# Two more places in the queue of small steps between a block's tokens and the turn of its normalised tokens

## The chip, the cores and the metric

The kernel runs on one core of one Trainium2 chip. The metric is the device time of one execution in microseconds (us), where lower is better. Each kernel is run several times; the time before is the median of three runs. One further execution was recorded by the hardware profiler, and everything said here of engines, waits and orders comes from that record.

The engines are named as the profile names them: PE (TensorE, the matrix unit), PEld (its weight loads), DVE (VectorE), ACT (ScalarE), POOL (GpSimd) and SP (SyncE, which here only issues transfers). [...]

## The reference

The input is four images of 128 channels by 4096 positions, in float32. Layer 0 group-normalises an image, makes queries and keys of 64 channels, values and a gate, attends over all positions, gates, projects and adds the input:

```python
vg = sigmoid(conv_bn(x, Wvg, svg, bvg)); v, gate = split(vg)
attn = softmax(einsum('bdn,bdm->bnm', q, k))
out = einsum('bcm,bnm->bcn', v, attn) * gate
x = x + conv_bn(out, Wp, sp, bp)
```

Layer 1 works on tokens (position by channel). It attends with queries that are their own keys, adds, normalises each token, and feeds the normalised tokens into a recurrence that runs over the positions:

```python
q = ln(t) @ W;  t = t + softmax(q @ q.T) @ ln(t)
Wx = batch_norm(ln(t) @ W_f.T)
y[n] = sigmoid(Wx[n] + y[n-1] @ V.T);  t = t + y
```

The queries of layer 1 are their own keys, so the score matrix is symmetric, and the kernel computes only half of its blocks.

## The kernel before, in words

All that counts here is in the function `fast`. For each of the four images it runs `layer0` and then `layer1`; after the last image comes the recurrence, as a scan over short pieces.

`layer0` goes over 8 blocks of 512 queries, each with 16 pairs of key tiles. A pair is two score matmuls (line 200), one exponential (ACT, line 202), a running sum (DVE, line 209) and four weighing matmuls (line 383).

`layer1` goes over the same 8 blocks in the order 6, 7, 5, 4, 3, 2, 1, 0, and in block n over the key blocks n, n-1, ..., 0. Each key block is two half steps. A half step is two score matmuls (line 573), two exponentials (ACT, line 579), two 32x32 block turns on DVE (line 584), and the two direct products of two half steps earlier (line 463). After a key block other than n itself, SP issues sixteen transfers that complete the turn of the scores (line 605). Some half steps later `reversed_products` uses the turned scores (four matmuls, line 476, a sum on DVE, line 481) for the mirrored block. So a query block is complete when its own products and all mirrored ones have arrived; then `finish(n)` runs.

Beside this main stream there are small steps, held in two queues. `pending` holds the steps that finish a block. `ahead` holds the 38 steps that prepare the next image for layer 0: four `stats`, `mean`, `variance`, and then per chunk of 512 positions `normalise`, `queries_keys`, `values` and `gate`. A half step of layer 1 takes one small step: the first of `pending`, or, if that is empty, the first of `ahead` (lines 598 to 601). Layer 0 takes from `ahead` first, then from `pending`, there in every second pair only, or in each pair while more than six are waiting (lines 215 to 218). The prepared image's queue is filled before its predecessor's layer 1 begins, and is empty in the last image.

`finish(n)` in layer 1 puts four steps into `pending`:

- `tokens`: the softmax sum's reciprocal, four PE transposes of the block into the tile `mt` (line 519), four DVE instructions that scale and add the old tokens into `t1b` (line 521), and a layer norm: statistics on DVE (lines 256, 257), the reciprocal root on POOL (lines 116, 117), and four DVE instructions that write the normalised tokens `h2` (line 260; the profile names this tile `h` or by its buffer).
- `result`: four PE transposes of `t1b` into `mr` (line 531), an ACT copy (line 533), a transfer to DRAM (line 534).
- `turn`: four PE transposes of the normalised tokens into `mh` (line 539), an ACT copy into `th` (line 540).
- `inputs`: one matmul of `th` into `mw` (line 544), statistics and a copy on DVE (lines 545, 551), a transfer to DRAM (line 552).

All small steps that need PSUM share one bank, the pool `ps_m`, which has one buffer under the one tag `m`: `mt`, `mr`, `mh`, `mw`, and `mp` of the steps for the next image (`queries_keys` at line 315, read by DVE 319, ACT 323 and DVE 327; `values` at 335, read by DVE 340; `gate` at 350, read by ACT 351).

The source order is not the final one. A scheduler reorders instructions on each engine when the program is built, following the dependencies, the buffers and its own idea of durations. So an edit of the source can move instructions that it doesn't mention.

The function `nothing` is a place holder. Layer 0 already uses it twice in its own list of finishing steps (line 430), where it does nothing and costs a place.

## Time and profile before

| | |
|---|---|
| median of three runs | 3160.87 us (3160.32 to 3160.97) |
| profiled execution: span | 3157.6 us |
| PE busy | 3071.5 us, 97% |
| DVE busy | 1792.3 us, 57% |
| ACT busy | 1128.2 us, 36% |
| POOL busy | 141.4 us, 4% |

The span is counted from the first to the last instruction. A matmul of 512 float32 columns appears as two records. The records overlap, [...] so the distance from one start to the next tells more than the length of a record. A line of the profile gives a source line, an engine, the tiles written and read, a count, the busy time with the mean of one, and after the bar the time that the engine was idle before these instructions and what ended that time.

### The profile page before, as it was taken

How to read it: one execution, taken by the hardware profiler on the slowest of the kernel's cores; microseconds unless marked ns; L12 is line 12 of the kernel's file. 1: busy time of each engine (PE TensorE's matmuls, PEld its weight loads, DVE VectorE, ACT ScalarE, POOL GpSimd, SP SyncE). 2: the span in 40 equal slices, each digit the busy share in tenths (PEclk: the TensorE clock that was granted, in tenths of full speed). 3: DMA queues.
4: the chain of work that ended last, by engine and by line, in shares of the span. 5: the costliest groups of instructions: out<-in, count | busy, mean ns of one | idle time of the engine just before them, and what ended most of it. 6: DMA issues, size and time to landing. Idle time of an engine off the chain costs nothing.

```text
span 3157.6 us, 32263 instructions
## 1 busy us (share of the span) xinstructions
PE 3071.5 (97%) x10770; PEld 1374.8 (44%) x10770; DVE 1792.3 (57%) x2964; ACT 1128.2 (36%) x1986; POOL 141.4 (4%) x183
## 2 busy tenths in 40 slices
PE   7999999999999999999999999999999999999976
PEld 3444444444444444444444444444444444444433
DVE  6555556555555555655555555555555655454546
ACT  3433333333333333333333333333333333223324
POOL 0000000000000000000000000000000000000000
PEclk9999999999999999999999999999999999999988
DMA  1111133333111123334211113333321112443324
GB/s 50 37 44 54 54 100 93 92 90 92 48 50 51 54 70 91 96 87 98 70 54 51 54 45 98 93 93 93 88 53 54 54 48 72 136 105 89 98 87 169
DMA packets 233167, 241.14 MB, mean 76 GB/s; under 512 B 88480, under 2 KB 144288, under 8 KB 231968
## 3 DMA queue, kind: packets, MB, share of 16 engines
q1 hardware_dynamic: 231984, 238.18, 27.2%
q8 instruction: 89, 1.46, 0.2%
q10 hardware_dynamic: 1008, 0.79, 0.1%
q14 instruction: 86, 0.70, 0.1%
HBM read 65.80 MB, written 56.62 MB: 39 GB/s over the span
## 4 chain that ended last, share of the span: by engine, by line
PE 91%; DVE 4%; POOL 1%; DMA 1%; SPq 1%; issue 1%; ACT 1%; ACTq 0%; DVEq 0%; POOLq 0%
PE o L383 28%; PE ps L200 15%; PE o L463 14%; PE ps L573 13%; PE ot L476 12%; PE mt L409 1%; PE mq L424 1%; PE mw L544 1%; PE md L227 1%; PE mp L315 1%; PE ps_r L719 1%; PE mh L539 1%; POOL rstd L117 1%; DVE t1b L521 1%; PE mp L350 1%
## 5 line engine op out<-in xcount | busy, mean ns | idle before, releaser
L383 PE MATMUL o<-e,nxt 64*128 64x512 f32 x4096 | 963.8, 589 | 0.0
L202 ACT ACTIVATE e<-ps 128x1024 f32<-128x1024 f32 x512 | 521.2, 1024 | 742.7 <-PE ps L200 738.1
L209 DVE TENSOR_TENSOR acc<-acc,e 128x1024 f32<-128x1024 f32 x448 | 546.4, 1220 | 387.9 <-ACT e L202 376.6
L579 ACT ACTIVATE e<-ps,shift 128x512 f32<-128x512 f32 x580 | 394.0, 684 | 776.4 <-PE ps L573 486.2
L383 PEld LDWEIGHTS o<-e,nxt 64*128 64x128 f32 x4096 | 398.9, 187 | 482.4 <-issue 474.6
L573 PE MATMUL ps<-qt 128*128 128x512 f32 x1160 | 550.4, 595 | 3.0 <-ACT e L579 3.0
L200 PE MATMUL ps<-nxt 64*128 64x512 f32 x2048 | 540.9, 602 | 1.2 <-DVE nxt L327 0.9
L463 PE MATMUL o<-e,h 128*128 128x512 f32 x1160 | 537.0, 592 | 0.0
L476 PE MATMUL ot<-tt,h 128*128 128x512 f32 x888 | 401.5, 595 | 5.3 <-DMA tt<-dd 5.3
L584 DVE STREAM_TRANSPOSE dd<-e 128x512 f32<-128x512 f32 x444 | 286.1, 685 | 110.8 <-ACT e L579 57.3
L463 PEld LDWEIGHTS o<-e,h 128*128 128x128 f32 x1160 | 218.4, 190 | 262.1 <-issue 261.2
L573 PEld LDWEIGHTS ps<-qt 128*128 128x128 f32 x1160 | 213.2, 191 | 244.4 <-issue 224.2
L200 PEld LDWEIGHTS ps<-nxt 64*128 64x128 f32 x2048 | 189.5, 186 | 248.0 <-issue 162.7
L476 PEld LDWEIGHTS ot<-tt,h 128*128 128x128 f32 x888 | 168.3, 191 | 217.1 <-issue 212.4
L481 DVE TENSOR_REDUCE slots<-tt 128x4 f32<-128x2048 f32 x111 | 250.6, 2258 | 11.3 <-DMA tt<-dd 11.2
L490 DVE TENSOR_TENSOR oacc<-oacc,ot 128x512 f32<-128x512 f32 x87 | 59.3, 682 | 209.5 <-PE ot L476 209.5
L116 POOL TENSOR_SCALAR rstd<-mv 128x4 f32<-128x4 f32 x64 | 14.6, 228 | 2519.5 <-DVE mv L257 2519.5
L579 ACT ACTIVATION_READ_ACCUMULATOR e<-ps,shift 128x1 f32 x580 | 113.9, 196 | 0.0
L401 POOL TENSOR_SCALAR xb<-xb,bpc 128x512 f32<-128x512 f32 x32 | 54.3, 1698 | 318.0 <-DMA xb<-in_x_dram 285.2
L117 POOL TENSOR_TENSOR rstd<-rstd,mhalf 128x4 f32<-128x4 f32 x64 | 66.4, 1038 | 5.3
L719 PE MATMUL ps_r<-y,w 128*128 128x256 f32 x168 | 54.4, 443 | 9.8 <-ACT y L716 7.8
L260 DVE TENSOR_SCALAR h<-t,mv,rstd 128x128 f32<-128x128 f32 x128 | 35.7, 343 | 45.3 <-POOL rstd L117 45.3
(124 smaller groups left out, 1411.8 us busy)
## 6 DMA issues: line engine op xcount, KB each, us to landing
tt<-dd SPq DMA_DIRECT2D x1776, 64.0 KB, 2.0
turn_d<-d SPq DMA_DIRECT2D x96, 256.0 KB, 2.0
t_d<-t SPq DMA_DIRECT2D x64, 256.0 KB, 2.0
nxt<-in_x_dram SPq DMA_DIRECT2D x16, 512.0 KB, 5.8
xb<-in_x_dram SPq DMA_DIRECT2D x32, 256.0 KB, 2.9
t<-turn_d SPq DMA_DIRECT2D x128, 64.0 KB, 2.0
yt<-turn_d SPq DMA_DIRECT2D x128, 64.0 KB, 1.9
ht<-turn_d SPq DMA_DIRECT2D x128, 64.0 KB, 2.0
```

Of the source, the lines that this page charges most:

```text
L117: nc.gpsimd.tensor_tensor(dst, dst, mhalf[:, :n], ALU.pow)
L200: nc.tensor.matmul(ps[:, h, :], lhsT=lhsT, rhs=rhs, start=True, stop=True)
L202: nc.scalar.activation(e, ps, AF.Exp, scale=scale)
L209: nc.vector.tensor_tensor(acc, acc, e, ALU.add)
L383: nc.tensor.matmul(o[r], lhsT=v[rs, p + h * PAIRS, :], rhs=e[rs, h, :], start=(p == 0 and h == 0), stop=(p == PAIRS - 1 and h == 1),)
L463: nc.tensor.matmul(o, lhsT=h[:, NQ * a + 2 * i + half, :], rhs=e[:, half, :], start=(a == order(n)[0] and i == 0 and half == 0), stop=(a = ...
L476: nc.tensor.matmul(ot, lhsT=h[:, NQ * n + j, :], rhs=t[:, :, j, :, :].rearrange("q p k j -> q k p j"), start=(j == 0), stop=(j == NQ - 1),)
L481: nc.vector.tensor_reduce(slots[:, bass.ts(n, NQ), a], t.rearrange("q p b k j -> q b p (k j)"), AX.XY, ALU.add,)
L573: nc.tensor.matmul(ps[:, half, :], lhsT=qt[:, bass.ts(at, P)], rhs=qt[:, bass.ts(n, QB)], start=True, stop=True,)
L579: nc.scalar.activation(e[:, half, :], ps[:, half, :], AF.Exp, bias=shift, accum_out=slots[:, at, n : n + 1],)
L584: nc.vector.transpose(d.rearrange("q f b k j -> q k b f j")[:, 2 * i + half], e[:, half, :].rearrange("q (b f j) -> q b f j", b=NQ, f=NQ),)
L719: nc.tensor.matmul(bank(k, s), lhsT=wt["vt"], rhs=before, start=False, stop=True, skip_group_check=True,)
```

## The change

Two edits. The place holder `nothing` now runs the first step of `ahead`, if there is one. And `finish` of layer 1 puts two such place holders between `result` and `turn`; in the last image only for the blocks 4 to 7.

```diff
         def nothing():
-            pass
+            if ahead:
+                ahead.popleft()()
...
                 if b == B - 1 and n == 0:
                     pending.extend([tokens, turn, inputs, result])
+                elif b == B - 1 and n < 4:
+                    pending.extend([tokens, result, turn, inputs])
                 else:
-                    pending.extend([tokens, result, turn, inputs])
+                    pending.extend([tokens, result, nothing, nothing, turn, inputs])
```

No instruction is added or removed on any engine; all that changes is their order. The place holders in layer 0's own list change too: where they come up in layer 1, at the start of an image's second layer, they also run a step of `ahead`.

## The prediction

> **What bounds the kernel now.** I read the page first, then who waits for whom on PE, then the timeline of PE around single turns.

> ```profile
> span 3157.6 us, 32263 instructions
> ...
> PE 3071.5 (97%) x10770; PEld 1374.8 (44%) x10770; DVE 1792.3 (57%) x2964; ACT 1128.2 (36%) x1986; POOL 141.4 (4%) x183
> ...
> PE 91%; DVE 4%; POOL 1%; DMA 1%; SPq 1%; issue 1%; ACT 1%; ACTq 0%; DVEq 0%; POOLq 0%
> ```

> The chain that ends last (third line) runs on PE for 91% of the span. No PE instruction is removed, so only PE's pauses can be won, and PE is idle for 86.1 us (3157.6 - 3071.5) in all, start and end included. The list of PE's waits says where:

> ```profile
> PE mh L539 <- DVE h L260: 15.7, 21, 4.4
> PE gm L292 <- DVE gmv L290: 14.2, 1, 14.2
> ...
> PE ot L476 <- DMA tt<-dd: 5.3, 3, 3.0
> PE ps L573 <- ACT e L579: 3.0, 6, 0.8
> PE mh L539 <- ACT e L579: 2.8, 3, 1.0
> ```

> The turn's transposes (line 539) waiting for the layer norm's last DVE step (line 260) are the largest entry. The second is one wait at the program's start. The timeline of image 0's block 7 shows one turn:

> ```profile
> 597.63 0.60 PE L531 MATMUL mr<-ident,t1b 128*128 128x128 f32 x4
> ...
> 598.07 1.88 PE L463 MATMUL o<-e,h 128*128 128x512 f32 x4
> ...
> 599.03 1.04 POOL L117 TENSOR_TENSOR rstd<-rstd,mhalf 128x4 f32<-128x4 f32 x1
> ...
> 600.10 1.11 DVE L260 TENSOR_SCALAR h<-t1b,mv,rstd 128x128 f32<-128x128 f32 x4 [1.48 <-POOL rstd L117]
> ...
> 600.60 0.49 PE L539 MATMUL mh<-ident,h 128*128 128x128 f32 x2 [0.65 <-DVE h L260]
> ```

> PE has four matmul records (1.72 us at 0.43 from start to start) for the time in which POOL takes the root and DVE writes the first normalised quarter. They end at 599.79 and the turn starts at 600.60: 0.81 us lost. From `result`'s first transpose to the turn's first is 2.97 us here and 2.1 to 3.3 us in image 0's other stalled turns; that is the distance needed.

> [...] records of 592 ns start 429 ns apart, so I count from start to start. [...] so one waiting transpose holds the main stream behind it, as at 600.60. [...] one queries/keys result is read by DVE (0.80 us), ACT (0.77) and DVE (0.82), one after the other. [...]

> **The change part by part.** Nothing is removed or added on any engine; the built program holds the same instructions in another order, and layer 0 of image 0 is untouched.

> *Moved later: `turn` and `inputs`.* Four transposes (0.11 us apart, 0.44), an ACT copy (0.59), a matmul of two passes (0.86), DVE statistics and copy (0.69 each), one transfer. None costs more at its new place, except that one group per image more falls between layer 0's matmuls, where a change of shape costs about 0.09 us on each side (520 against 429 ns): 0.2 us an image, 0.6 in all. On SP the transfer of line 552 stands 32 instead of 16 score transfers behind that of line 534. [...] PE waited for scores 3 times only (5.3 us), all in image 3 before its first `finish`, where this transfer doesn't exist. I take nothing.

> *The gain.* In the built order of PE I count the matmuls between `result` and `turn` at 0.43 us a pass. Image 0, in order of blocks 6, 7, 5, 4, 3, 2: before 1.9, 1.9, 1.9, 1.9, 1.1, 1.9 us; after 9.7, 5.4, 10.5, 6.2, 7.9, 9.7. All exceed the 3.3 us needed. Start to start, those six turns lost, with the gaps between their transposes, 0.85, 0.8, 0.95, 0.85, 0.8 and 1.1: 5.35 us. Blocks 1 and 0 lose nothing before (5.4 us of work). Block 7 keeps about 0.5 (next part). So 4.8 us an image, 14.4 for three. In image 3 the built order separates block 6 (8.8 us) and block 7 (4.5) but leaves 1.9 us in blocks 5 and 4, although their places were moved: 0.85 + 0.75 won, 1.6. Sum 16.0 us.

> *Moved earlier: the next image's steps.* They now use the bank between `result` and `turn`. The bank is free about 1.1 us after `mr`'s end, and about 1.0 after a gate's. In two turns an image the step follows with 0.86 us of work, 0.2 us each; the old order had two such gate pairs as well, so I put 0.2 more. In block 7's turn `queries_keys` comes in, and its reads stand behind the layer norm on DVE: first read at about 3.6 us after `mr`'s start (600.10 + 1.11 - 597.63), the three reads done at 6.0, where PE comes to `turn` at 5.6 to 5.9: the 0.5 kept above covers these. ACT's read waits as well, with exponentials behind it for about 2.9 us; PE has two score buffers and some 3.4 us of work, so I add nothing.

> *The cluster of the first chunks.* With the queue two or more places further on, its order changes about 40 us into layer 1. Before, PE lost time there so:

> ```profile
> 476.81 1.12 PE L573 MATMUL ps<-qt 128*128 128x512 f32 x2 [0.76 <-ACT e L579]
> ...
> 484.23 2.84 PE L573 MATMUL ps<-qt 128*128 128x512 f32 x6 [0.25 <-ACT e L579]
> ...
> 487.37 1.16 PE L335 MATMUL mp<-w,nxt 128*128 128x128 f32 x8 [0.29 <-DVE nxt L340]
> ```

> Start to start these are 0.92, 0.42 and 0.46: 1.8 us, 1.9 with small gaps. In the new order a `values` group stands directly behind a `queries_keys` matmul, with no PE work between. These lines price it:

> ```profile
> 477.77 1.02 PE L315 MATMUL mp<-nxt,w 128*128 128x512 f32 x2
> ...
> 478.83 0.80 DVE L319 TENSOR_SCALAR nxt<-mp,par 64x512 f32<-64x512 f32 x1 [2.03 <-PE mp L315]
> ...
> 479.67 0.77 ACT L323 ACTIVATE nxt<-mp,par 64x512 f32<-64x512 f32 x1 [2.91 <-DVE nxt L319]
> ...
> 480.48 0.82 DVE L327 TENSOR_SCALAR nxt<-mp,par 64x512 f32<-64x512 f32 x1 [0.84 <-ACT nxt L323]
> ```

> From the second pass's end (478.63) to the third read's end (481.30) are 2.7 us, in which PE now stands. With 0.3 for exponentials in a queue, the cluster costs 3.0 us: 1.1 more an image, 3.3 for three. Bounds: below, the DVE queue may run ahead and the whole cluster cost no more than before (0); above, the two score waits come on top (1.3 more an image).

> *Layer 0's edge.* Image b+1's first block now ends while a transpose of image b's last block still holds the buffer of `og`, so line 392 starts about 0.6 us later. In the trace the block's two sums are freed 2.1 us after the last weighing matmul; with 0.6 added this meets PE's need for a third buffer at about 2.9. Zero taken, at most 0.7 an image.

> *The steps that fall into layer 0's old place holders* (two `stats`) stand at the same place on DVE as before, the scheduler having drawn them ahead already. The mean and variance chain moves before a score turn on DVE (line 584), which may start about 3 us later; DVE was idle 8.9 us just before it. Zero.

> Sum: 16.0 - 0.6 - 0.6 (the 0.2 for gates, three images) - 3.3 = 11.5 us, so the profiled span would be 3146. The three runs lie about 3.3 us above the span; the difference is set off against their median: 3160.9 - 11.5 = 3149.4, rounded 3149.

> **The rivals.**
> - *Whole gain.* The cluster costs what it did, and block 7's turn waits for nothing: 16.0 + 1.5 - 0.6 = 17, so 3144. For it: DVE is busy 57% only. Against: the serial three reads are in the trace.
> - *The wait moves to the bank.* The new users of the one bank take back most of it: the cluster at its upper bound (4.0 more in three images), layer 0's edge at its bound (2.1), 0.5 more for blocked exponentials in each of three turns (1.5): 11.5 - 7.6 = 4, so 3157. For it: ACT's order puts exponentials behind a read that waits for DVE.
> - *Slower, by starved scores.* If an exponential queued behind a small step's read holds up the score matmuls for 1.5 us in each of the six turns of three images (18 turns, 27 us), the sum is 15 us slower, 3176. It decides from 0.64 us a turn (11.5 / 18). For it: PE waited for exponentials for up to 0.8 us in the old cluster. Against: in the turns ACT is 36% busy and there are matmuls of 3 us and more between.
> - *The change does nothing where meant.* The built order leaves blocks 5 and 4 of image 3 as they were; for images 0 to 2 it does separate them, so only that remainder (1.7 us) stays.

> **How the numbers follow.** Chances: forecast (3146 to 3153) 0.55, whole gain (3141 to 3146) 0.17, moved wait (3153 to 3161) 0.20, slower 0.08. About 0.2%, 6.3 us, is what a measurement of this kernel can tell from no change. Faster than 3154.5 takes the first two and a fifth of the third: 0.76. The rest of the third is same, 0.16; slower 0.08. The range leaves out half of the whole gain's case at its far end, a little of the moved wait's, and the slower case: 3142 to 3160. The forecast's own range is 3146 to 3153.

> **What would show it.** Right: line 539's idle time falls from 18.5 us to about 7 (the last block's 4.4 us, block 5 and 4 of image 3 and a little of block 7), PE's busy time is unchanged, and a wait of lines 335 or 315 for DVE line 327 appears, 2 to 3 us in each of three images. Wrong: the idle time of line 539 stays; or scores (line 573) wait for ACT for more than 6 us in all; or `ot` waits for transfers in images 0 to 2.

## The result, and the profile after

The changed kernel takes 3147.1 us (median of four runs, 3144.93 to 3148.81) against 3160.85 (3160.32 to 3160.97): 13.75 us less, a ratio of 0.9956 with an interval of 0.9939 to 0.9974. The profiled execution spans 3144.8 us, 12.8 less than that of before. Lines after line 170 of the source stand 3 further down now, those after the second edit 5: the turn's transposes are line 542, the layer norm's last step 263, the bank's third read 330, `values` 338, the scores 578.

The page of the kernel after: span, busy time, and the chain that ends last.

```profile
span 3144.8 us, 32242 instructions
...
PE 3064.3 (97%) x10770; PEld 1379.2 (44%) x10770; DVE 1798.6 (57%) x2964; ACT 1125.5 (36%) x1986; POOL 142.0 (5%) x183
...
PE 94%; DVE 3%; SPq 1%; DMA 1%; POOL 0%; ACT 0%; issue 0%; ACTq 0%; DVEq 0%; POOLq 0%
```

The same 10770 matmuls run, and PE's share of the chain rises from 91% to 94%: what went away is standing time. PE's busy time fell by 7.2 us, where the prediction had it unchanged. The record of a pass is longer than the distance to the next start (592 against 429 ns), so up to 0.16 us of each pause counts as busy; of the 12.8 us only 5.6 show as idle time (80.5 us, before 86.1). Who waits for whom on PE (total us, times, longest):

```profile
PE mp L338 <- DVE nxt L330: 7.7, 3, 2.6
PE mh L542 <- DVE h L263: 6.5, 4, 4.4
...
PE ot L479 <- DMA tt<-dd: 4.7, 3, 3.0
```

The turn's wait (18.5 us with the part that was put down to ACT) is down to 6.5, of which 4.4 are the last block of all. The waits of scores for ACT (3.0 us in six places) are off the list of the costliest. A new entry stands above the turn's: `values` waits for the third read of the small bank, once in each of the first three images. The timeline of PE around block 7's turn in image 0:

```profile
596.04 0.60 PE L534 MATMUL mr<-ident,t1b 128*128 128x128 f32 x4
596.47 1.02 PE L466 MATMUL o<-e,h 128*128 128x512 f32 x2
597.35 1.12 PE L318 MATMUL mp<-nxt,w 128*128 128x512 f32 x2
598.32 1.88 PE L578 MATMUL ps<-qt 128*128 128x512 f32 x4
600.03 1.88 PE L466 MATMUL o<-e,h 128*128 128x512 f32 x4
602.05 0.66 PE L542 MATMUL mh<-ident,h 128*128 128x128 f32 x4
```

Twelve passes stand between `mr` and `mh` where there were four, the bank's new user (line 318) among them, and the distance is 6.0 us. The last product before the turn needs 1.72 us from start to start, and the turn starts 2.02 us after it (602.05 - 600.03), so 0.3 us are still lost: the bank holds the turn up, whose first weight load waits 0.97 us for the third read (line 330). The place of the new wait, in image 0, all engines but PEld:

```profile
489.12 1.07 PE L318 MATMUL mp<-nxt,w 128*128 128x512 f32 x2
490.23 0.80 DVE L322 TENSOR_SCALAR nxt<-mp,par 64x512 f32<-64x512 f32 x1 [1.22 <-PE mp L318]
491.07 0.77 ACT L326 ACTIVATE nxt<-mp,par 64x512 f32<-64x512 f32 x1 [2.91 <-DVE nxt L322]
491.88 0.82 DVE L330 TENSOR_SCALAR nxt<-mp,par 64x512 f32<-64x512 f32 x1 [0.84 <-ACT nxt L326]
...
492.75 1.16 PE L338 MATMUL mp<-w,nxt 128*128 128x128 f32 x8 [2.56 <-DVE nxt L330]
```

Three reads, one after the other, and nothing for PE to do: this is the sequence that the prediction priced at 2.7 us. It is 2.56 us of idle time; counted from start to start 2.72 are lost. The third read takes the other 64 partitions than the second and still waits for ACT (0.84 us in the trace); what asks for that isn't shown.

In image 1 the same pause has a sequel. The timeline of PE there:

```profile
1238.06 1.07 PE L318 MATMUL mp<-nxt,w 128*128 128x512 f32 x2
1241.68 1.32 PE L338 MATMUL mp<-w,nxt 128*128 128x128 f32 x8 [2.56 <-DVE nxt L330]
1242.80 5.17 PE L479 MATMUL ot<-tt,h 128*128 128x512 f32 x8
```

Eight records of `ot` take 5.17 us; eight such records take 3.60 elsewhere. The table of stretches of 3.41 us around the pause names the cause: the first two are of image 0, the next two of image 1, the last two of image 2 (after the times: length, busy time of PE, PEld, DVE, ACT and POOL with counts, TensorE's granted clock with 1.00 for the full one, DMA share, GB/s).

```profile
488.19:491.60 3.41, 2.00 (x5) 0.49 (x3) 1.62 (x2) 0.53 (x1) 0.00 (x0) 1.00 0.45 109
491.60:495.01 3.41, 2.26 (x11) 1.57 (x12) 1.88 (x3) 0.58 (x2) 0.00 (x0) 1.00 0.24 58
1239.13:1242.54 3.41, 0.86 (x7) 0.86 (x8) 1.62 (x2) 0.77 (x1) 0.00 (x0) 1.00 0.41 100
1242.54:1245.95 3.41, 3.41 (x7) 1.61 (x6) 2.90 (x3) 0.63 (x1) 0.00 (x0) 0.50 0.02 5
1990.06:1993.47 3.41, 1.17 (x9) 1.17 (x10) 1.34 (x2) 0.77 (x1) 0.00 (x0) 1.00 0.39 96
1993.47:1996.88 3.41, 3.41 (x5) 1.38 (x5) 3.38 (x3) 0.63 (x1) 0.00 (x0) 0.50 0.02 5
```

In images 1 and 2 the granted clock falls to half for 3.4 us, beginning about 1 us after the pause's end. In image 0 the pause is as long, and the clock stays. The last section returns to these lines.

The cleanest measure of what each kernel wins is the time from the first score of one image's layer 1 to that of the next image's, called an image's time from here on. Before it is 754.2 us in each of three images; now it is 748.9 us in image 0 and 750.6 in images 1 and 2, where the half clock costs 1.7.

### The profile page after: what moved, and what is told of

Its sections match the earlier page's. It is cut to its first block, busy times and chain, and to the rows that moved or that the text cites. A ratio compares the mean times of both kernels' runs of the same rounds, so it can differ in the third digit from the quotient of the medians.

```text
span 3144.8 us, 32242 instructions
## 1 busy us (share of the span) xinstructions
PE 3064.3 (97%) x10770; PEld 1379.2 (44%) x10770; DVE 1798.6 (57%) x2964; ACT 1125.5 (36%) x1986; POOL 142.0 (5%) x183
## 4 chain that ended last, share of the span: by engine, by line
PE 94%; DVE 3%; SPq 1%; DMA 1%; POOL 0%; ACT 0%; issue 0%; ACTq 0%; DVEq 0%; POOLq 0%
PE o L386 28%; PE ps L578 15%; PE o L466 15%; PE ps L203 15%; PE ot L479 12%; PE mq L427 1%; PE mt L412 1%; PE md L230 1%; PE mw L547 1%; SPq L610 1%; PE ps_r L724 1%; PE mp L318 1%; PE mp L338 1%; PE mp L353 1%; PE mh L542 1%; DVE ps_r L711 1%
## 5 line engine op out<-in xcount | busy, mean ns | idle before, releaser
L484 DVE TENSOR_REDUCE slots<-tt 128x4 f32<-128x2048 f32 x111 | 250.7, 2258 | 11.7 <-DMA tt<-dd 11.6
L116 POOL TENSOR_SCALAR rstd<-mv 128x4 f32<-128x4 f32 x64 | 14.4, 225 | 2525.0 <-DVE mv L260 2525.0
L117 POOL TENSOR_TENSOR rstd<-rstd,mhalf 128x4 f32<-128x4 f32 x64 | 66.4, 1037 | 5.3
```

Of the source, the lines that this page charges most:

```text
L117: nc.gpsimd.tensor_tensor(dst, dst, mhalf[:, :n], ALU.pow)
L484: nc.vector.tensor_reduce(slots[:, bass.ts(n, NQ), a], t.rearrange("q p b k j -> q b p (k j)"), AX.XY, ALU.add,)
```

## The experiments

The change is two edits at once: places between a block's tokens and its turn, and work drawn forward into them and into layer 0's old place holders. The theory at this point: the distance between `result` and `turn` is the gain, the work in the places is not needed for it, and the bank wait comes from where the next image's steps now fall. The rival: the work that fills the places is itself a gain, as it fills PE's pauses and clears the queue. The kernel before stood at 3160.92, 3160.77 and 3160.64 us in the three sittings.

| kernel | median, us (range) | ratio to before [95%] | profiled span |
|---|---|---|---|
| two places, empty | 3146.47 (3145.06 to 3146.89) | 0.9951 [0.9938, 0.9965] | 3144.7 |
| filled place holders, none in layer 1 | 3157.45 (3156.0 to 3159.67) | 0.9989 [0.9983, 0.9996] | 3154.6 |
| two filled, layer 0's own empty | 3144.28 (3144.04 to 3145.7) | 0.9947 [0.9934, 0.9961] | 3142.3 |
| the same, three in the last image | 3141.9 (3141.53 to 3142.78) | 0.9939 [0.9926, 0.9953] | 3139.8 |
| the change with a shorter bank hold | 3139.44 (3137.47 to 3143.68) | 0.9937 [0.9924, 0.9951] | 3135.7 |
| before, turn made of the old tokens | 3133.08 (3132.26 to 3133.75) | 0.9913 [0.99, 0.9927] | 3130.9 |
| one place | 3147.48 (3146.98 to 3149.83) | 0.996 [0.9947, 0.9974] | 3147.0 |
| shorter hold, three in the last image | 3136.96 (3136.01 to 3139.6) | 0.9923 [0.9909, 0.9936] | 3137.9 |

### Two places, both empty

```diff
         def nothing():
-            if ahead:
-                ahead.popleft()()
+            pass
```

> The two places stand between result and turn as in the change, but the place holder does nothing, so no step of the next image is drawn forward. My theory (the gain is the turn's wait for the layer norm, no more): the built order sets 9.0, 4.7, 3.0, 3.0, 5.6 and 14.2 us from result to turn in each of the first three images, and 3.0 is just enough, so line 539's waits there vanish (5.3 us an image) and those of blocks 6 and 7 of image 3 (1.7). The old cluster of the first chunks (1.8 us an image) stays as it was; two pairs of gates come closer (0.6 us each): 3 x (5.3 - 1.0) + 1.7 = 14.6 us faster, about 3146. Rival (the gain is the next image's work, done earlier in the places): nothing drawn forward, nothing won, 3160.

3146.47 us, beside the change's 3147.1 and inside its range. The waits of PE in this kernel (its lines are those of before, plus 2 behind the second edit):

```profile
PE mh L539 <- DVE h L260: 6.5, 4, 4.4
...
PE ps L575 <- ACT e L581: 3.0, 6, 0.8
```

The turn's wait falls to the same 6.5 us as with the change. There is no wait for the bank's third read, the scores' old waits are there as in the kernel before, and there is no stretch at half clock in images 0 to 2 (the mean granted clock of the profiled execution is 0.993, with the change 0.991). So the distance by itself gives nearly all of the gain, and as the main cause the rival falls. That the work drawn forward gives nothing at all does not follow, since in the change its own costs, the bank's wait and the half clock, are set off against it. An image's time is 750.4 us here; where the two places are filled without those costs (two filled, layer 0's own empty, below) it is 749.5. Filling is thus worth 0.9 us an image. A likely reason, not tested apart: four groups of `gate` an image stand between layer 0's matmuls here and none there, so that matmuls of 64 and of 128 rows follow each other 74 times against 66. From one such matmul to the next of the other kind the traces show about 520 ns, where 429 are usual; as an estimate from these figures, eight changes fewer are worth 0.7 us.

### Filled place holders, but none in layer 1's list

```diff
-                    pending.extend([tokens, result, nothing, nothing, turn, inputs])
+                    pending.extend([tokens, result, turn, inputs])
```

> The place holder runs a step of the next image, but no place is put between result and turn; it acts through layer 0's own list alone. My theory: line 539 waits as before (5.3 us an image), and the order of the first chunks is the new one, with values directly behind queries_keys: a wait of line 335 for line 327 of 2.7 us in each of three images in place of the old cluster's 1.8, so 2 to 3 us slower than before, about 3163. Rival (next image's work drawn forward is the gain): about 3147.

3157.45 us, where about 3163 was expected: a miss. The waits of PE:

```profile
PE mh L542 <- DVE h L263: 14.9, 21, 4.4
...
PE mp L338 <- DVE nxt L330: 7.7, 3, 2.6
```

The bank's wait is here at full size, so layer 0's two place holders make it: they now take two steps of `ahead` at the start of layer 1 and shift the whole queue. The turns still wait. The miss comes from two things. The new pause was expected to cost more than the old pauses that it replaces; in this trace those (scores for ACT, and `values`) are gone, and the exchange comes out nearly even. And in block 2 a new order of the built program leaves no wait: the timeline of PE in image 0 shows

```profile
787.16 0.60 PE L534 MATMUL mr<-ident,t1b 128*128 128x128 f32 x4
787.60 1.88 PE L578 MATMUL ps<-qt 128*128 128x512 f32 x4
789.32 0.60 PE L542 MATMUL mh<-ident,h 128*128 128x128 f32 x4
```

with the turn 2.16 us behind `mr` and ready. Image 0's turns lose 4.3 us here from start to start, 5.7 in the kernel before. An image's time is 752.1 us in images 0 and 2, and 754.1 in image 1, the only one with the half clock behind the bank's wait (eight records of `ot` take 5.30 us there); before it is 754.2.

### Two filled places, layer 0's own place holders empty

```diff
-            [sums, projection, nothing, tokens, nothing, queries]
+            [sums, projection, lambda: None, tokens, lambda: None, queries]
```

> The change as it is, but layer 0's own two place holders stay empty; only the two new places in layer 1 are filled. My theory (the 2.7 us wait comes from layer 0's place holders, not from the new places): the wait of line 335 for line 327 vanishes, the old cluster of 1.8 us comes back instance for instance, the turns are separated (12.5, 3.9, 5.6, 4.7, 5.6, 9.9 us), and block 7's turn keeps no wait for the bank: 0.9 + 0.3 us an image better than the change, about 3143.5. Rival (the wait comes from the new places): the 7.7 us of line 335 stay, time as the change, 3147.

3144.28 us against 3143.5 expected. The wait for line 330 is gone from the list, the scores' old waits are back, and no half clock follows in images 0 to 2 (mean granted clock 0.993):

```profile
PE mh L542 <- DVE h L263: 6.5, 4, 4.4
...
PE ps L578 <- ACT e L584: 3.0, 6, 0.8
```

Together with the run before it this settles where the bank's wait comes from. Why it is faster is another matter. Its image's time is 749.5 us in all three images; the change's is 748.9 where the clock stays full and 750.6 where it falls. So without the half clock the change's order, with the bank's wait, is 0.6 us an image faster, not 1.2 slower as expected here (block 7's turn still waits 0.3 us, now for the read of `values`), and what this kernel saves is the half clock. That the time came out as expected is luck. In all, the first three images are 1.5 us shorter than with the change; the rest of the 2.5 us between the profiled spans lies outside them. The median is 2.8 us under the change's; its range meets the change's (3144.04 to 3145.7 beside 3144.93 to 3148.81), and the two ran in different sittings, so the profile carries this more than the times.

### The same, with three places in the last image

```diff
-                    pending.extend([tokens, result, nothing, nothing, turn, inputs])
+                    pending.extend([tokens, result] + [nothing] * (3 if b == B - 1 else 2) + [turn, inputs])
```

> As the previous kernel, with three places instead of two in the last image's blocks 4 to 7, where the built order then sets 12.4, 11.6, 5.6 and 10.7 us between result and turn (two places left 2.1 us in two of the four). My theory: the two waits of line 539 for line 260 that the change left in image 3 (0.8 us each) vanish, 1.6 us faster than the previous kernel, about 3142; what is left of that line's waits is the last blocks' 5 us. Rival (image 3 has slack elsewhere, as its waits for transfers show): no difference from the previous kernel.

```profile
PE mh L542 <- DVE h L263: 5.2, 2, 4.4
```

3141.9 us, as expected. In the last image `ahead` is empty, so a place only moves the turn; with a third one, blocks 5 and 4 lose nothing either, and the four waits of PE for the turn become two. That is 2.4 us under the kernel with two, where the two blocks' waits were 1.6; in the traces the last image, from its first score in layer 1 to its last product, is 2.0 us shorter.

### The change with a shorter hold of the bank

ACT makes the second half of `q` from the first half in SBUF, and reads the bank no more:

```diff
                 nc.vector.tensor_scalar(
                     q[lo, cs], m[lo, :], ...
-                nc.scalar.activation(q[hi, cs], m[lo, :], AF.Identity, bias=..., scale=...)
                 nc.vector.tensor_scalar(
                     k[lo if ch < 4 else hi, bass.ts(ch % 4, 512)], m[hi, :], ...
+                nc.scalar.copy(q[hi, cs], q[lo, cs])
```

> The change with one edit in queries_keys: the second half of the queries is copied by ACT from the first half in SBUF instead of being computed from the shared PSUM bank, so the bank has two reads (DVE 0.80, DVE 0.82) and not three. In the built order values still stands directly behind queries_keys. My theory (PE stands there for as long as the bank is read, and a pause of about 2.6 us is what brings the stretches of 3.4 us at half the TensorE clock, 1.7 us each, behind it): the wait falls from 2.6 to about 1.8 us in each of three images, and no half-clock stretch follows it: 3 x 0.8 + 2 x 1.7 = 5.8 us under the change's profiled span of 3144.8, and 3141 to 3144 in the timed runs. Rival A (half-clock stretches come by themselves, whatever the pause): the waits shorten by 2.4 us in all and the stretches stay, 3145. Rival B (the wait is for something other than the reads of the bank): no difference, 3147.

3139.44 us, below the expected 3141 to 3144. The timeline of image 0 at this place:

```profile
488.29 0.80 DVE L322 TENSOR_SCALAR nxt<-mp,par 64x512 f32<-64x512 f32 x1 [2.04 <-PE mp L318]
489.13 0.82 DVE L326 TENSOR_SCALAR nxt<-mp,par 64x512 f32<-64x512 f32 x1
...
490.09 1.13 PE L335 MATMUL mp<-w,nxt 128*128 128x128 f32 x8 [1.84 <-DVE nxt L326]
```

The pause is 1.84 us instead of 2.56, by ACT's 0.77 less. And in image 1, where the change had its half clock:

```profile
1237.87 1.13 PE L335 MATMUL mp<-w,nxt 128*128 128x128 f32 x8 [1.84 <-DVE nxt L326]
1238.84 3.60 PE L476 MATMUL ot<-tt,h 128*128 128x512 f32 x8
```

Eight records of `ot` take 3.60 us again, and the granted clock is 1.00 from 1238.0 to 1245.0 us. An image's time is 747.8 us in all three images, together 6.9 us less than with the change. Nearly all of it has a place: 2.2 for the shorter pause (0.72 us, three times), 3.4 for the two stretches of half clock that no longer follow, and 1.1 because block 7's turn no longer waits for the bank either. So both rivals fall in this trace. The medians are 7.7 us apart, with ranges of 6.2 and 3.9. The profiled span is 9.1 us shorter, but part of that lies at the program's start, which the edit reaches too: the first score starts at 23.6 us (24.5 in the later kernel with this edit, 25.6 to 27.0 in the others), and layer 0 of image 0 gives back 1.5.

### Before, with the turn made of the old tokens

This prices the wait by itself. The turn transposes `t1b`, which is ready with `result`, instead of the normalised tokens; the recurrence so gets tokens without their layer norm.

```diff
-                        ... h2[:, j, :] ...
+                        ... t1[:, j, :] ...
```

> The kernel before, with turn transposing the tokens t1b instead of the normalised tokens h2; so what goes into the recurrence is not normalised, and the layer norm is still computed but nothing waits for it. It prices the wait of line 539 by itself. My theory: the wait is worth 5.4 us in each of three images, 3.3 in blocks 6, 7, 5 and 4 of the last and 3 to 4 in its last blocks, so 22 to 24 us faster than before, 3137 to 3139; the old cluster of the first chunks stays. Rival (PE's pauses at line 539 would come up elsewhere, since DVE or ACT carry the next limit): less than 12 us faster.

3133.08 us, 27.7 under before, and lower than the expected 3137 to 3139. In the traces an image's time falls by 6.2 us in each of the first three images, of which 5.6 are the turns' own pauses. The last image, from its first score in layer 1 to its last product, is 4.8 us shorter, and what follows that product 3.0. That makes 26.5 of the 26.7 us between the profiled spans, so the rival falls. The images were expected at 5.4 and 3.3 us, which is most of the miss. The last 3.0 us the change leaves as they are: its last block still waits 4.4 us. The list of waits for the two entries that matter:

```profile
PE ps L573 <- ACT e L579: 3.0, 6, 0.8
...
PE mh L539 <- DVE t1b L521: 1.3, 1, 1.3
```

### One place instead of two

```diff
-                    pending.extend([tokens, result, nothing, nothing, turn, inputs])
+                    pending.extend([tokens, result, nothing, turn, inputs])
```

> The change with one place between result and turn instead of two. The built order then sets 3.9, 2.1, 3.9, 3.0, 3.9 and 6.4 us between result and turn in the first three images, and 2.1 in all four blocks of the last. My theory (3.0 us is what the layer norm needs): block 7 waits 0.8 us in each image, image 3's four blocks wait as before, the other turns do not; the 2.7 us wait for the bank is as in the change. So 0.5 us an image and 1.6 in the last one worse than the change: about 3150. Rival (one place is a full half step of 5 us and so enough): as the change, 3147.

```profile
PE mh L542 <- DVE h L263: 9.5, 9, 4.4
...
PE mp L338 <- DVE nxt L330: 7.7, 3, 2.6
```

The profile shows nine waits instead of four, 3.0 us more of them, and a span 2.2 us longer. But the longer wait of block 7 costs nothing in the sum: an image's time is within 0.02 us of the change's in each of the first three images, since the change's pause at the start of layer 0 (0.4 us) and its waits before gates (0.3) don't come up with one place. Here the rival holds. The last image is 2.9 us longer than with the change: 1.7 for the turns of blocks 6 and 7, which wait again, the rest in the main for waits of `ot` for transfers (6.6 us in all, with the change 4.7). The medians, 3147.48 and 3147.1, don't separate the two kernels, and neither do their ranges.

### Shorter hold and three places in the last image

```diff
-                nc.scalar.activation(q[hi, cs], m[lo, :], AF.Identity, bias=..., scale=...)
+                nc.scalar.copy(q[hi, cs], q[lo, cs])
...
+                    pending.extend([tokens, result] + [nothing] * (3 if b == B - 1 else 2) + [turn, inputs])
```

> The previous kernel with two reads of the bank in queries_keys, and three places instead of two in the last image's blocks 4 to 7, where the built order then sets 12.4, 11.6, 5.6 and 10.7 us between result and turn. My theory: the waits of line 539 in blocks 5 and 4 of the last image (0.8 us each) vanish on top, 1.6 to 2.4 us under 3139.4, about 3137.5. Rival (image 3's waits for transfers take it back): 3139.5.

3136.96 us, the fastest of the kernels that compute the whole: 10 us under the change, 24 under before. Its list of waits joins the two parts: the bank's wait is 5.5 us in all instead of 7.7, and the turn's is 5.2 (twice) instead of 6.5 (four times). How little of a difference one trace settles is seen here too: its profiled span (3137.9) is longer than that of the kernel with two places (3135.7), since a half-clock stretch of 6.8 us fell into its last image in that execution (mean granted clock 0.992, there 0.993), while its median is 2.5 us lower.

## Why the prediction was right

The mechanism was the one that it named: the turns' wait for the layer norm goes, and a wait for the small bank's third read comes. Its sum was 2 us too careful against the timed median (11.5 us forecast, 13.75 measured), and that it came so close is partly luck. Point by point, for one image of the first three. Measured is what PE's pauses (each distance between two starts less the usual one of that shape) grew or shrank by in image 0 between the two traces:

| step | forecast, us | measured, us |
|---|---|---|
| turns | -4.8 | -5.25 |
| cluster of the first chunks | +1.1 | +0.5 |
| gates and other users of the one bank | +0.2 | -0.6 |
| layer 0: one more group (0.2, by changes of shape), and its edge | +0.2 | +0.7 |
| pauses under 0.1 us each | 0 | -0.7 |
| sum | -3.3 | -5.3 |
| half clock, in images 1 and 2 only | 0 | +1.7 |

- *The turns.* Right in place and size. The counts of passes in the built order, 5.4 to 10.5 us, came out as 6.0 to 11.0 in the trace. All turns but block 7's (0.36 us, forecast 0.5) lose nothing beyond 0.06. In the last image blocks 6 and 7 were freed (1.7 us, forecast 1.6), and 5 and 4 kept 1.6, as the built order said; another 1.3 us of pauses beside transfers and weighing matmuls went there, which the prediction hadn't counted.
- *The cluster.* The new pause was forecast at 3.0 us and is 2.7, with 0.2 of small gaps in the group itself. The 0.3 for queued exponentials didn't come. The mis-sized term is the old cluster: counted at 1.9 us from three lines of the timeline, it is 2.4 when every distance between scores is summed (1.3 of waits between scores, 0.7 ahead of `values`, 0.4 behind it). The miss of the run with filled place holders alone had in part the same cause.
- *Gates and the one bank.* The new gate pairs wait (0.17 us) as forecast, but older waits of this kind vanished: `mw`'s two passes lost 0.43 us and lose 0.1, and the gates' total fell by 0.2.
- *Layer 0's edge.* Taken at nothing, bounded at 0.7. There is a pause of 0.4 us at the start of layer 0 in each of three images, which the kernel before doesn't show.
- *Scores, transfers, place holders in layer 0.* Taken at nothing, and seen as nothing: waits of scores for ACT went down instead of up, `ot` waits for transfers 4.7 us instead of 5.3, and still only in the last image. The rival of starved scores is refuted by this.
- *The half clock.* Not foreseen at all. It took back 3.4 us in the profiled execution.

Summed, the first three images became 5.3, 3.6 and 3.6 us shorter and the last one, up to its last product, 3.0: 15.5 us. The span shrank by only 12.8, for two stretches in which the change moves nothing: the first score starts 1.1 us later in that execution (26.96 us, before 25.9), and the part after the last product is 1.6 us longer (112.0, before 110.4). Why that part is longer isn't shown. So the forecast erred on both sides, and the errors cancelled in part: without the half clock the four images would have won 18.9 us (15.5 + 3.4), 7.4 more than the 11.5; the half clock took back 3.4, and the start and the end of that execution 2.7. As an estimate from these figures: if the timed runs had two such stretches each, as the profiled one, the median without them would be near 3144, the whole gain's number and outside the forecast's own 3146 to 3153.

The rival of the whole gain (3144) is 3.1 us from the median, the forecast (3149) 1.9. The rival's condition isn't met: the three reads do stop PE for their whole length, and only because the old pauses were larger than counted does the exchange come near even. The rival of a moved wait had the place right; its extra costs, scores and exponentials, didn't come.

## What to carry to other kernels

In block 7's turn before, PE stood for 0.81 us at a waiting transpose, with the next scores (line 573) behind it. So price such a dependent pair by the work of the engine between producer and consumer in the built program, here some 3 us between `result` and `turn`; a place in a queue wins it, and what fills the place is a question of its own. A helper that two lists share changes both: the gain came from one list and the new wait from the other. A pause on the bounding engine costs its length, and here half clock came behind 12 of the 23 pauses of 2.56 us or more, at about 1.7 us a stretch in images 1 and 2. Shortening what holds a shared buffer won both here: half clock followed none of the pauses of 1.84 us.

## What the runs showed of the hardware that was not expected

| pause of PE | half clock begins at its end (from 1.1 us before to 1.4 us behind) |
|---|---|
| 1.33 to 1.84 us | 0 of 12 |
| 2.56 us (the bank's wait) | 5 of 9 (the change 2 of 3, filled place holders alone 1 of 3, one place 2 of 3) |
| 2.9 to 3.2 us (a transfer, last image) | 7 of 14 |

A stretch costs about 1.7 us of work done late (750.6 against 748.9 us for an image). Equal pauses so ended differently, and the six lines under "The result" show one thing that differed. In image 1 PE is idle for 2.55 of the 3.41 us right before the half clock, in image 2 for 2.24. In image 0 the two stretches have 1.41 and 1.15 us of idle time, and nothing follows. They are laid to match the half clock of the other images: in this trace the stretches of images 1, 2 and 3 begin 750.93 and 737.28 us apart, 220 and 216 times 3.4133 us to within 0.01, and image 0's are counted back from there in the same steps. The two half-clock stretches beside transfers look like those of images 1 and 2: in the 3.41 us before them PE is idle for 2.61 us (the change, from 2727.34 us) and 2.50 (before, from 2739.58). After the shorter waits for a transfer in the same image (1.51 and 1.55 us), where such a stretch has 1.26 and 1.21 us, the clock stays at 1.00. That the place of the pause within these steps makes the difference is the author's reading of two traces; no run tested it.

That the bank's wait brings the half clock the runs without it show: the stretches in images 0 to 2 go when the wait is taken away (layer 0's place holders empty) or shortened to 1.84 us, and the mean granted clock of the profiled execution is 0.993 in both, 0.991 with the change. How often half clock came in the timed runs without a trace stays open.
